# Written-out engine order at the end of a nearest-row search, a moved staging tile, and rank-order products in bf16 pieces

## The chip, the cores and the metric

The kernel runs on one core of one Trainium2 chip. The metric is device time of one execution in microseconds (us). The time before is the median of four runs: 1054.99 us (1054.68 to 1055.5). The hardware profiler took one further execution; the tables, timelines and chains quoted here are of that execution.

A core has these engines, each with its own instruction queue: PE (matrix products into PSUM, with PEld for the weight loads), DVE (vector work), ACT (activation functions and copies), POOL (GpSimd: elementwise work, and the issue of indirect transfers) and SP (which here only issues transfers). Each queue is executed in order. An instruction that waits holds up everything behind it on its own engine.

## What is computed

Four graph layers on N = 2708 nodes with D = 128 features and a dense weighted adjacency matrix A (2708 x 2708). The change touches the first two layers.

```
# layer 0
z    = leaky(d1 * (A @ (d1 * x)) @ W1 + b1)         # d1 = rowsum(A)^-1/2
S    = exp(-dist(z, z)/2), kept for the 4 nearest rows of each row
d2   = rowsum(S + A)^-1/2
x    = layernorm(x + d2 * ((S + A) @ (d2 * x)) @ W2 + b2)
# layer 1
den  = exp(leaky(r[:, None] + c[None, :]))          # r, c: one number per node
att  = den / (A @ den)
x    = layernorm(x + A @ (att @ (x @ W)))
# layers 2 and 3: two more products with A, each with a small weight and a layernorm
```

## The kernel before

**Tiling.** Rows are cut into T = 22 tiles of 128 (the last has 20 rows), columns into C = 6 chunks (four of 512, one of 384, one of 276). The first S = 16 row tiles of A are streamed through a ring buffer, the last six stay on the chip.

**The search** (L676 to L708). For each row tile PE builds 2708 keys in PSUM, ACT copies them into a `key` buffer (three buffers), and DVE takes the eight largest (`max`, L701) and their places (`max_index`, L702). Tiles go in the order 4 to 15, 0 to 3, 16 to 20; tile 21 is handled apart. A scheduler decides the order of each engine's instructions in this loop.

**The search's end.** `weigh` (L591) turns distances into weights (`sim`), sums them into the second degree, takes its inverse root `d2inv`, forms `y2 = d2inv * x`, and writes `y2` to the DRAM rows `y2_rows`. It is called for tiles 0 to 16, 17 to 19, and 20 to 21. `others` (L562) sets the own row apart from the three other near rows; it runs on POOL for the first two groups and on DVE for the last. After that, `add_bias` (L264) adds b2 to all of `xs` in one DVE instruction of 2816 elements per partition.

**Pass 2** is the product of A with `y2`, column chunk by chunk (L204 in `by_panels`). A `Due` list, which ticks once per product, says after how many products each side job is emitted; PE, DVE and ACT run in that written order. `sum_near` (L733) sums near rows of `y2`: for each tile POOL issues three indirect gathers (`gather_near`, L729) from `y2_rows`, and DVE adds them up with weights (L742). The job for tile t is due at tick 24 + 23t/5. When a chunk's product is complete and its near rows are there, `end_pass2` emits at tick n: `add_near` (L749, near rows into the same PSUM bank), a copy by ACT, the product with W2 (`norm0`, L780), normalisation, and the comparisons that rank the nodes by c (`compare` L884, `rank_rows` L902, `rank_columns` L907).

**The rank stage** (L1080 to L1475) follows. Each node has a rank in the order of c. Three things run beside each other, by a list `turns` written by hand: (1) `line` and `own_line`, products of a 32-column weight `lc` with half rows of A that are loaded into berths; when a line was used, its berth is loaded with a later one (L1032). (2) the rank-order products `in_rank_order` (L1201, output `js`): a 0/1 matrix `hot`, made on DVE by comparing (L1191), times `val_q`, which holds for each node its number and its c in f32; this sorts nodes by c. (3) `find_blocks` on DVE, then `counts` on PE (L1287), then `find_places`, then `in_list_order` (L1201, output `sl`), which gives the row lists (`slot_i`) with which POOL gathers rows of A for the attention loop, and `next_weights` for its weights `lw`. At the end `end_half(1)` copies column sums out of PSUM into the second half of the tile `heads`, and `send_half` sends them to the tile `carry` by four transfers of SP (L1389).

**The attention loop** (`block_layer`, from L1590). 44 steps; in each PE forms `num` (L1627), ACT inverts it by Ln and Exp (L1481, L1484), DVE corrects it in three instructions (L1491, L1495, L1498), and PE adds up the result (`hacc`, L1506). The buffers `inv` and `err` come from a pool that is opened after the rank stage's pool `rank` is closed, and lies where that pool lay; the first instruction that writes there waits until everything in the old pool is read, `heads` included.

Of the kernel before, what the change touches and what calls it, by code (L numbers as in the profile page):

```python
# [8 lines left out]
F32 = mybir.dt.float32  # L9
U32 = mybir.dt.uint32  # L10
I32 = mybir.dt.int32
BF16 = mybir.dt.bfloat16
# [40 lines left out]
def kernel(  # L53
# [310 lines left out]
    with tc.tile_pool(name="knn", bufs=1) as knn:  # L364
# [226 lines left out]
        def weigh(ts):  # L591

            t0, t1 = ts[0], ts[-1] + 1
            nr, sm = near[:, t0:t1, :TOPK], sim[:, t0:t1, :]

            nc.vector.tensor_add(nr, nr, nsq[:, t0:t1, None].to_broadcast([P, t1 - t0, TOPK]))
            nc.vector.tensor_scalar(nr, nr, 0.0, DIST_EPS, op0=ALU.min, op1=ALU.subtract)
            nc.scalar.activation(sm, nr, AF.Ln, scale=-1.0)
            nc.scalar.activation(sm, sm, AF.Exp, scale=0.5)
            nc.scalar.activation(sm, sm, AF.Exp, scale=-0.5)  # L600
            dd = d2inv[:, t0:t1]
            nc.vector.tensor_reduce(dd, sm, AX.X, ALU.add)
            nc.vector.tensor_add(dd, dd, deg[:, t0:t1])  # L603
            nc.scalar.activation(dd, dd, AF.Ln)
            nc.scalar.activation(dd, dd, AF.Exp, scale=-0.5)
            if t1 < T:
                nc.gpsimd.tensor_mul(
                    y2[:, t0:t1, :], xs[:, t0:t1, :], d2inv[:, t0:t1, None].to_broadcast([P, t1 - t0, D])
                )
# [5 lines left out]
            queue.dma_start(  # L615
                y2_rows[t0 * P : full * P, :].rearrange("(t p) d -> p t d", p=P), y2[:, t0:full, :]
            )
            if full < t1:
                queue.dma_start(y2_rows[FULL * P :, :], y2[:LAST, FULL, :])
            else:  # L620
                for a in range(t0, t1, 11):
                    others(range(a, min(a + 11, t1)), nc.gpsimd)
# [50 lines left out]
        tc.keep_in_program_order(nc.scalar.preload_act_table_set("natural_log_exp_and_others"))  # L673
        with tc.tile_pool(name="keys", bufs=3) as keys:

            for n, t in enumerate([*range(4, S), *range(4), *range(S, FULL)]):  # L676
# [18 lines left out]
                for c in range(C) if n else (5, 3, 2, 4, 1, 0):  # L695
# [78 lines left out]
    add_bias(b2_sb)  # L774
# [266 lines left out]
    val_q = lwx.tile([P, T, 3, NQ], F32, tag="xws", name="val_q")  # L1041
# [35 lines left out]
    with tc.tile_pool(name="rank", bufs=1) as rank:  # L1077
# [20 lines left out]

        find_ranks()
# [87 lines left out]
        def ones_at(at, n, order=iota):  # L1187
            t0, t1 = parts[n]
            w = t1 - t0
            hot = hot_in[:, n % 3 * 6 * P : (n % 3 * 6 + w) * P].rearrange("p (t k) -> p t k", k=P)  # L1190
# [15 lines left out]
        in_q = val_q[:, :, 2, :]  # L1206
# [4 lines left out]
        for n, v in enumerate((node_oob, cc)):  # L1211
            nc.vector.tensor_mul(val_q[:, :, n, :], in_q, v[:, :, None].to_broadcast(grid_q))

        places = row_tile("hot_in")
        hot_in = places[:, : 3 * 6 * P]
        two_b = places[:, 3 * 6 * P :].bitcast(BF16)[:, : T * NB].rearrange("p (t b) -> p t b", b=NB)
        assert (T * D - 3 * 6 * P) * 2 >= T * NB
        hot = [ones_at(b_j, n) for n in range(3)]

        def ranked(js):  # L1220
# [154 lines left out]
        def end_half(h):  # L1375
# [3 lines left out]
            tot = heads[:, h * span : (h + 1) * span]  # L1379
# [26 lines left out]
        def in_rank_order(n):  # L1406
            into_places(work["js"], hot[n], val_q[:, :, :2, :], n)
# [27 lines left out]
        heads = rtile([2 * span], "heads")  # L1435
# [11 lines left out]
        def own_line(n):  # L1447
# [12 lines left out]
            (next_weights,), (own_line, 1), (next_weights,), (line, 2), (next_weights,),  # L1460
            (own_line, 1), (next_weights,), (line, 1), (next_weights,), (own_line, 1), (line, 1), (next_weights,),
            (line, 1), (add_last_rows, 1), (own_line, 2),
        ]
        for f, *args in turns:
            f(*args)
        end_half(1)
# [5 lines left out]
        send_half(1, heads[:, span:], nc.sync)  # L1472
# [41 lines left out]

    m_rows = row_tile("m_rows").rearrange("p (t d) -> p t d", d=D)
    mT = m_rows.rearrange("p t d -> p (t d)")[:, :N]
# [304 lines left out]
```

## Time and profile before

| what | value |
|---|---|
| time, median of four runs | 1054.99 us |
| profiled execution: own time | 1056.77 us |
| profiled execution: span of the instructions | 1055.0 us |
| PE busy | 984.7 us, 93% |
| DVE busy | 637.3 us, 60% |
| ACT busy | 331.4 us, 31% |
| POOL busy | 264.9 us, 25% |
| mean granted TensorE clock | 0.969 |

The profiled execution lasted 1.77 us longer than its span; that is what lies before the first and after the last instruction. The stages follow each other: degrees and first product up to about 150 us of the span, the search to 290, pass 2 to about 440, the rank stage to 497, the attention loop to 720, then three products with A to the end. Shares of busy time are means over these stages, so they do not tell what an edit in one stage is worth. For that one reads, in the stage, which engine is never idle, where it does stand idle, and what ended that idle time: in a timeline this stands in brackets at the end of a line, as "[us idle <-releaser]". The granted clock is given by stretches of time as a share of full speed.

### The profile page before, as it was taken

The numbers are of one execution on the slowest core, as the hardware profiler recorded it, in microseconds if no ns is written. First come the engines' busy times: TensorE is split into PE (matmuls) and PEld (weight loads), VectorE is DVE, ScalarE is ACT, GpSimd is POOL, SyncE is SP. The second block draws the span as 40 slices with busy tenths as digits, with TensorE's granted clock in tenths as the row PEclk, the third lists the DMA queues.
The fourth block names the chain that finished last, engine by engine and source line by source line (L and its number), as shares of the span: only waits on it lengthen the run. The fifth ranks groups of instructions, "written<-read, shape, count | busy, mean of one in ns | idle before, by whom it ended". The sixth has DMA issues, their size and how long they took to land.

```text
span 1055.0 us, 11657 instructions
## 1 busy us (share of the span) xinstructions
PE 984.7 (93%) x3773; PEld 483.9 (46%) x3773; DVE 637.3 (60%) x1358; ACT 331.4 (31%) x609; POOL 264.9 (25%) x339
## 2 busy tenths in 40 slices
PE   0898999999997998799899999999999999999996
PEld 0345554444444556555333333334445544564444
DVE  5885437999954677764899999994121121122222
ACT  0000115555601244602777776662010100010000
POOL 4000000000377674007666444330121100000000
PEclk9898999999998998699899999999999999999998
DMA  9999360000075766597465556556665956585652
GB/s 339 346 365 256 97 197 1 0 1 1 1 247 194 239 176 195 195 410 232 131 181 145 141 142 160 145 160 218 217 194 171 302 176 219 146 270 163 224 173 69
DMA packets 102001, 191.00 MB, mean 181 GB/s; under 512 B 14022, under 2 KB 43342, under 8 KB 101930
## 3 DMA queue, kind: packets, MB, share of 16 engines
q1 hardware_dynamic: 83896, 152.34, 43.9%
q0 software_dynamic: 17728, 37.62, 13.0%
q8 instruction: 32, 0.52, 0.2%
q14 instruction: 39, 0.32, 0.1%
q10 hardware_dynamic: 306, 0.20, 0.1%
HBM read 214.80 MB, written 4.16 MB: 208 GB/s over the span
## 4 chain that ended last, share of the span: by engine, by line
PE 49%; DVE 1%; ACT 1%; issue 0%; POOL 0%; POOLq 0%; DVEq 0%
PE acc L204 28%; PE hacc L1506 10%; PE num L1627 10%; PE mis L285 1%; PE mis L1756 0%; DVE inv L1495 0%; DVE err L1491 0%; ACT gb L234 0%; PE mis L1722 0%; DVE inv L1498 0%; PE mis L1752 0%; POOL rstd L253 0%; PE mis L1710 0%; ACT m_rows L160 0%; DVE xs L277 0%
## 5 line engine op out<-in xcount | busy, mean ns | idle before, releaser
L1068 POOL DMA_INDIRECT ring<-in_adjT,slot_i x88 | 93.5, 1062 | 96.2 <-PE num L1627 77.4
L1627 PE MATMUL num<-ring,lw 128*64 128x512 f32 (+1 forms) x528 | 112.7, 560 | 5.1 <-DVE err L1491 4.4
L1506 PE MATMUL hacc<-inv,xws 128*128 128x512 f32 (+1 forms) x264 | 112.0, 560 | 0.3 <-DVE inv L1498 0.3
L699 PE MATMUL acc<-zT,z 128*128 128x512 f32 (+2 forms) x252 | 102.2, 552 | 0.0
L1481 ACT ACTIVATE inv<-num,plain 128x1024 f32<-128x1024 f32 x88 | 80.6, 916 | 59.5 <-PE num L1627 42.0
L253 POOL TENSOR_TENSOR rstd<-rstd,minus_half 128x4 f32<-128x4 f32 (+1 forms) x18 | 17.3, 960 | 311.8 <-DVE rstd L252 311.8
L234 ACT COPY gb<-acc 128x512 f32<-128x512 f32 (+2 forms) x18 | 9.6, 534 | 249.4 <-PE acc L204 249.4
L700 ACT COPY key<-acc 128x512 f32<-128x512 f32 (+2 forms) x126 | 67.0, 534 | 55.2 <-issue 28.0
L1506 PEld LDWEIGHTS hacc<-inv,xws 128*128 128x128 f32 x264 | 46.8, 191 | 78.0 <-issue 34.5
L204 PE MATMUL acc<-ring,y 128*128 128x512 f32 (+2 forms) x192 | 82.0, 558 | 0.5 <-issue 0.5
L1491 DVE TENSOR_TENSOR err<-inv,num 128x1024 f32<-128x1024 f32 x88 | 74.7, 854 | 10.8 <-SPq L1817 8.2
L729 POOL DMA_INDIRECT got<-y_rows,where x66 | 71.4, 1082 | 27.0 <-issue 9.1
L1498 DVE SCALAR_TENSOR_TENSOR inv<-gb,g_inv,inv 128x1024 f32<-128x1024 f32 x88 | 77.0, 914 | 0.1
L204 PE MATMUL acc<-ring,xs 128*128 128x512 f32 (+2 forms) x192 | 76.7, 543 | 0.0
L204 PE MATMUL acc<-ring,carry 128*128 128x512 f32 (+2 forms) x192 | 74.5, 542 | 0.0
L204 PE MATMUL acc<-ring,m_rows 128*128 128x512 f32 (+2 forms) x192 | 74.3, 542 | 0.0
L1495 DVE SCALAR_TENSOR_TENSOR inv<-err,inv 128x1024 f32<-128x1024 f32 x88 | 72.4, 861 | 0.1
L699 PEld LDWEIGHTS acc<-zT,z 128*128 128x128 f32 x252 | 45.9, 190 | 50.3 <-issue 44.9
L575 POOL TENSOR_TENSOR slot_e<-near,sim 128x44 f32<-128x44 f32 (+2 forms) x3 | 0.7, 242 | 270.0 <-DVE d2inv L603 267.9
L1484 ACT ACTIVATE inv<-inv 128x1024 f32<-128x1024 f32 x88 | 67.6, 768 | 2.8
L1627 PEld LDWEIGHTS num<-ring,lw 128*64 128x64 f32 x528 | 36.5, 138 | 62.5 <-issue 44.4
L701 DVE MAX8 near<-key 128x8 f32<-128x2708 f32 x21 | 62.3, 2965 | 2.6 <-ACT key L700 2.6
(376 smaller groups left out, 1374.4 us busy)
## 6 DMA issues: line engine op xcount, KB each, us to landing
ring<-in_adjT SPq DMA_DIRECT2D x74, 1024.0 KB
ring<-in_adjT SPq DMA_DIRECT2D x20, 677.0 KB
ring<-in_adjT SPq DMA_DIRECT2D x17, 768.0 KB
part<-in_adjT SPq DMA_DIRECT2D x12, 1024.0 KB
ring<-in_adjT SPq DMA_DIRECT2D x17, 552.0 KB
more<-in_adjT SPq DMA_DIRECT2D x10, 677.0 KB
res<-in_adjT SPq DMA_DIRECT2D x4, 1280.0 KB
part<-in_adjT SPq DMA_DIRECT2D x3, 768.0 KB
```

The lines of the kernel that those rows point to most:

```text
L204: nc.tensor.matmul(accs[c][: lhsT.shape[-1], :w], lhsT=lhsT, rhs=src, start=start, stop=stop)
L699: nc.tensor.matmul(pks[c][:p, : cw[c]], lhsT=z2[:, :p], rhs=zT[:, cs], start=False, stop=True)
L700: nc.scalar.copy(key[:p, cs], pks[c][:p, : cw[c]])
L729: nc.gpsimd.indirect_dma_start(out=got[:p, :], out_offset=None, in_=y2_rows[:, :], in_offset=bass.IndirectOffsetOnAxis(ap=where[:p, t, k : ...
L1068: nc.gpsimd.indirect_dma_start(out=rows[i][:KC, n, :], out_offset=None, in_=adj_half[:, :], in_offset=bass.IndirectOffsetOnAxis(ap=slot_i[ ...
L1481: nc.scalar.activation(inv, num[:, :w], AF.Ln, scale=plain[:, 0:1], bias=plain[:, 1:2])
L1484: nc.scalar.activation(inv, inv, AF.Exp, scale=-1.0)
L1491: nc.vector.tensor_mul(err, inv, num[:, :w])
L1495: nc.vector.scalar_tensor_tensor(inv, err, 2.0, inv, op0=ALU.subtract, op1=ALU.mult)
L1498: nc.vector.scalar_tensor_tensor(inv, gb[:, col : col + w], g_inv[:, q : q + 1], inv, op0=ALU.max, op1=ALU.mult)
L1506: nc.tensor.matmul(haccs[:, o:e], lhsT=xws[:, q, :], rhs=inv[:, o:e], start=(q == 0), stop=(q == NQ - 1))
L1627: nc.tensor.matmul(num[n * (BJ + 2) : (n + 1) * (BJ + 2), o:e], lhsT=lw[:, 2 * q + n, :], rhs=rows[i][:, n, c0 + o : c0 + e], start=True, ...
```

## The change

1. **The search's end.** `weigh` is cut into `weigh_near`, `find_d2` and `keep_y2`. Distances are now worked on in `sim` instead of in place in `near`. From tile 16's `max` on, DVE runs in the written order. `weigh_near` stands between a tile's `max` and its `max_index`; the rest for tiles 0 to 16 and 17 to 19 stands behind `max_index`; for tiles 20 and 21 everything up to the write of `y2` stands ahead of tile 20's `max_index`. For tiles 17 to 19, `y2` and its write are now emitted ahead of `others`.
2. **The bias.** The one addition of 2816 elements is replaced by one addition per chunk in pass 2 (`add_b2`). The due ticks of `sum_near` change from 24 + 23t/5 to 20 + 24t/5.
3. **The rank-order products.** The node number is split into two bf16 pieces and c into three (six new POOL instructions on 22 elements per partition). `val_q` becomes bf16 with five values, `hot` becomes bf16 for these products, the products are 110 columns wide instead of 44, and `ranked` adds the pieces up again (one ACT copy, three DVE instructions).
4. **The turns.** The first three rank-order products stand together, and `counts` stands after two lines instead of after eight; the lines go behind it. A few later lines and weights are in another order.
5. **The staging tile.** The second half of `heads` is no longer in the pool `rank` but in `m_rows`, a tile of the outer pool.

```diff
+                if t == T - 6:
+                    ends.enter_context(tc.manual_schedule(engines={nc.vector.engine}))
                 nc.vector.max(near[:p, t, :], key[:p])
+                if t == T - 6:
+                    weigh_near(range(0, T - 5))
+                if t == T - 3:
+                    weigh_near(range(T - 5, T - 2))
+                if t == T - 2:
+                    weigh_near(range(T - 2, T))
+                    others(range(T - 5, T - 2), nc.gpsimd)
+                    find_d2(range(T - 2, T))
+                    keep_y2(range(T - 2, T))
                 nc.vector.max_index(where[:p, t, :], near[:p, t, :], key[:p])
+                if t == T - 3:
+                    find_d2(range(T - 5, T - 2))
+                    keep_y2(range(T - 5, T - 2))
                 if t == T - 6:
-                    weigh(range(0, T - 5))
-                if t == T - 3:
-                    weigh(range(T - 5, T - 2))
-            weigh(range(T - 2, T))
+                    find_d2(range(0, T - 5))
+                    keep_y2(range(0, T - 5))
+                    for a in range(0, T - 5, 11):
+                        others(range(a, min(a + 11, T - 5)), nc.gpsimd)
             others(range(T - 2, T), nc.vector)
+            ends.close()
...
-    add_bias(b2_sb)
...
-    near_at = [24 + (23 * t) // 5 for t in range(T)]
+    near_at = [20 + (24 * t) // 5 for t in range(T)]
+    def add_b2(ts):
+        rows = xs[:, ts[0] : ts[-1] + 1, :]
+        nc.vector.tensor_add(rows, rows, b2_sb[:, None, :].to_broadcast([P, len(ts), D]))
...
+    for ts in chunk_tiles:
+        at(near_at[ts[0]], add_b2, ts)
...
-    val_q = lwx.tile([P, T, 3, NQ], F32, tag="xws", name="val_q")
+    val_q = lwx.tile([P, T, 6, NQ], BF16, tag="xws", name="val_q")
...
+        nc.gpsimd.tensor_copy(parts_b[:, :, 0], node_oob)
+        nc.gpsimd.tensor_sub(parts_b[:, :, 1], node_oob, parts_b[:, :, 0])
+        nc.gpsimd.tensor_copy(parts_b[:, :, 2], cc)
+        nc.gpsimd.tensor_sub(rest, cc, parts_b[:, :, 2])
+        nc.gpsimd.tensor_copy(parts_b[:, :, 3], rest)
+        nc.gpsimd.tensor_sub(parts_b[:, :, 4], rest, parts_b[:, :, 3])
...
-        for n, v in enumerate((node_oob, cc)):
-            nc.vector.tensor_mul(val_q[:, :, n, :], in_q, v[:, :, None].to_broadcast(grid_q))
+        grid_q = [P, T, 5, NQ]
+        nc.vector.tensor_mul(
+            val_q[:, :, :5, :], in_q[:, :, None, :].to_broadcast(grid_q), parts_b[:, :, :, None].to_broadcast(grid_q)
+        )
...
-            nc.vector.tensor_scalar_add(row_j, js[:, :NQ], float(OOB))
-            nc.vector.tensor_copy(csort, js[:, NQ : 2 * NQ])
+            nc.scalar.copy(js_sb, js[:, : 5 * NQ].rearrange("p (v q) -> p v q", q=NQ))
+            nc.vector.scalar_tensor_tensor(
+                row_j, js_sb[:, 0], float(OOB), js_sb[:, 1], op0=ALU.add, op1=ALU.add
+            )
+            nc.vector.tensor_add(csort, js_sb[:, 2], js_sb[:, 3])
+            nc.vector.tensor_add(csort, csort, js_sb[:, 4])
...
-            (line, 4), (blocks_of_edges,), (line, 7), (last_xw,), (in_rank_order, 0), (line, 3),
-            (in_rank_order, 1), (line, 3), (in_rank_order, 2), (count_lone,), (line, 2), (counts,), (line, 3),
-            (add_last_rows, 0), (own_line, 4), (ranks_known,), (line, 2), (own_line, 1), (in_list_order, 0),
+            (line, 4), (blocks_of_edges,), (line, 7), (last_xw,), (in_rank_order, 0), (in_rank_order, 1),
+            (in_rank_order, 2), (line, 2), (count_lone,), (counts,), (line, 5), (add_last_rows, 0), (own_line, 4),
+            (ranks_known,), (line, 2), (own_line, 1), (in_list_order, 0),
...
-        heads = rtile([2 * span], "heads")
+        heads = [rtile([span], "heads")]
...
+        m_rows = row_tile("m_rows").rearrange("p (t d) -> p t d", d=D)
+        mT = m_rows.rearrange("p t d -> p (t d)")[:, :N]
+        heads.append(mT[:, HALF : HALF + span])
         end_half(1)
...
-        send_half(1, heads[:, span:], nc.sync)
+        send_half(1, heads[1], nc.sync)
```

More of the change, by code (lines that the diff above doesn't have):

```diff
@@ L605, in weigh, with keep_y2 @@
             nc.scalar.activation(dd, dd, AF.Exp, scale=-0.5)
+        def keep_y2(ts):
+            t0, t1 = ts[0], ts[-1] + 1
             if t1 < T:
@@ L619, in weigh @@
                 queue.dma_start(y2_rows[FULL * P :, :], y2[:LAST, FULL, :])
-            else:
-                for a in range(t0, t1, 11):
-                    others(range(a, min(a + 11, t1)), nc.gpsimd)
         QUARTER = N // 4
@@ L673 @@
         tc.keep_in_program_order(nc.scalar.preload_act_table_set("natural_log_exp_and_others"))
+        ends = ExitStack()
         with tc.tile_pool(name="keys", bufs=3) as keys:
@@ L1097, in on_all @@
                 nc.scalar.copy(row[:, n * P : n * P + e], ps[:, :e])
+        rest = spare[:, 3 * T : 4 * T]
+        parts_b = spare[:, 4 * T : 4 * T + (5 * T + 1) // 2].bitcast(BF16)[:, : 5 * T].rearrange("p (t v) -> p t v", v=5)
+        nc.gpsimd.tensor_copy(parts_b[:, :, 0], node_oob)
[4 more added lines that the diff above has]
+        nc.gpsimd.tensor_sub(parts_b[:, :, 4], rest, parts_b[:, :, 3])
         find_ranks()
@@ L1185, with ones_at @@
         parts = [(t, min(t + 6, T)) for t in range(0, T, 6)]
-        def ones_at(at, n, order=iota):
+        def ones_at(at, n, order=None):
             t0, t1 = parts[n]
             w = t1 - t0
-            hot = hot_in[:, n % 3 * 6 * P : (n % 3 * 6 + w) * P].rearrange("p (t k) -> p t k", k=P)
+            hot = hot_b[:, t0 * P : t1 * P] if order is None else hot_in[:, n % 3 * 6 * P : (n % 3 * 6 + w) * P]
+            hot = hot.rearrange("p (t k) -> p t k", k=P)
+            order = iota if order is None else order
             nc.vector.tensor_tensor(
@@ L1204, in into_places @@
                 )
-        in_q = val_q[:, :, 2, :]
+        in_q = val_q[:, :, 5, :]
         grid_q = [P, T, NQ]
@@ L1378, in end_half @@
                 carries.append(big.tile([P, NQ * P], F32, tag="y", name="carry"))
-            tot = heads[:, h * span : (h + 1) * span]
+            tot = heads[h]
             nc.scalar.copy(tot[:, : edges[4] - edges[3]], banks[h][:, : edges[4] - edges[3]])
@@ L1406, in in_rank_order @@
         def in_rank_order(n):
-            into_places(work["js"], hot[n], val_q[:, :, :2, :], n)
+            into_places(work["js"], hot[n], val_q[:, :, :5, :], n)
             if n == 2:
```

22 lines of the change are left out of this document (12 added, 10 removed).

## The prediction

> **What bounds the kernel now.** I read the page's busy table first, then the chain that ended last, then PE's waits, then PE's timeline and the stretches around each stage that the change touches.
>
> ```profile
> PE 984.7 (93%) x3773; PEld 483.9 (46%) x3773; DVE 637.3 (60%) x1358; ACT 331.4 (31%) x609; POOL 264.9 (25%) x339
> ```
>
> PE is busy 93% of the span and nearly the whole chain lies on it. So an edit pays in two ways only: PE stands for less time, or PE's own work gets shorter; a third, hidden one is the granted clock after a stand. The change touches three places where PE stands or works slowly, A, B and C.
>
> **A, the search's end and pass 2.** The columns of a timeline are start, length, engine, line, operation, count; the bracket is the idle time ahead and its releaser. PE:
>
> ```profile
> 323.25 0.83 PE L749 MATMUL acc<-ident,near_sum 128*128 128x128 f32 x6
> 329.45 0.79 PE L749 MATMUL acc<-ident,near_sum 128*128 128x128 f32 x2 [5.37 <-DVE near_sum L742]
> 330.03 3.62 PE L204 MATMUL acc<-res,y 128*128 128x512 f32 x4
> ```
>
> PE stands 5.37 us for the sum of tile 3, which needs the twelfth gather. Behind the stand four products last 3.62, 0.91 each, and the clock of 330 to 333 was 0.50; the 4.55 us up to 334.0 lost half, 2.3. POOL and DVE tell why the gathers are late:
>
> ```profile
> 301.22 3.07 POOL L585 CAST where<-near 128x9 uint32<-128x9 f32 x1
> 304.24 0.85 POOL L615 DMA_DIRECT2D y_rows<-y  x1
> ...
> 308.45 1.15 POOL L729 DMA_INDIRECT got<-y_rows,where  x1 [2.84 <-DMA y_rows<-y]
> ```
>
> ```profile
> 301.15 3.09 DVE L265 TENSOR_TENSOR xs<-xs,b 128x2816 f32<-128x2816 f32 x1 [1.61 <-POOL y L607]
> ```
>
> The cast of nine numbers lasts 3.07 (0.20 for eighteen at 295.18) because the bias addition runs beside it; the write of `y2` for tiles 17 to 19 stands behind it on POOL, the first gather behind the write.
>
> After: `others` of tiles 11 to 16 waits for ACT, in written order now, ahead of tile 17's `max`: about 2.5 us (one key copy of 0.53 and ACT's casts) that the old order hid. With `weigh_near` ahead of the indices, tile 20's `max` goes from 290.77 to about 296.3 end, the last `y2` to 298.4, its write's issue to 299.7. With 2.5 for landing (the gathers' shortest) the first gather starts at about 302.2, not 308.45; the write for tiles 17 to 19 is out by 296. `near_sum` of tile 3 came 20.9 after the first gather, so at 323.1. PE comes to it sooner too, since the tick is 37 instead of 40: 3 ticks of 0.865 earlier, at about 321.3 with the six additions. It stands 1.8: gain 3.6. The clock fell 3 us into the old stand; I count half of the 2.3 back, 1.1. Against it: `add_b2` of the last chunks (384 elements; by the row of 2816 in 3.09 about 0.45) now stands on DVE in the chain to `xT` (L801), where PE already stands 2.64 at 414.45, and one group of rank columns, 0.5, moves ahead of chunk 5's last product: −1.0. The other `add_b2` lie in DVE's idle time beside products. **A = 3.7.** Bounds: 0.3, if the gathers start 2.3 later and the clock falls; 6.7, if the whole stand and its slow clock go.
>
> The trace shows a POOL instruction as long as the DVE instruction beside it, 3.07 against 3.09. The Trainium skill's page "SBUF — State Buffer", section "Who interferes with whom", calls this an exclusive lock: a DVE instruction with two SBUF inputs and a GpSimd instruction that reads SBUF block each other for the whole instruction. This agrees with the cast and speaks against the change, since six two-input `add_b2` now stand among the gathers: by it each could hold a gather by 0.45, up to 1.8 for the four chunks ahead of tile 3's and later ones. The rows say otherwise: 28 gathers lasted 1.00 to 1.15 although 21 two-input sums of 0.35 ran among them, so the sum takes nothing for it.
>
> **B, the rank stage.** PE has no idle time there but for 1.03 us in 453 to 456; so here PE's own work counts, and its waits for DVE.
>
> ```profile
> 455.86 1.83 PE L1201 MATMUL js<-val_q,hot_in 128*128 128x44 f32 x12
> ...
> 460.80 1.53 PE L1201 MATMUL js<-val_q,hot_in 128*128 128x44 f32 x12
> ...
> 464.10 1.53 PE L1201 MATMUL js<-val_q,hot_in 128*128 128x44 f32 x12
> ...
> 467.03 0.38 PE L1287 MATMUL cnt<-in_b,upper_b 128*128 128x484 bf16 x1
> ...
> 468.01 1.86 PE L1287 MATMUL mis<-hot_in,ones_b 128*128 128x484 bf16 x11
> 469.72 0.44 PE L1294 MATMUL mis<-hot_in,ones_b 128*128 128x44 bf16 x11
> ```
>
> The f32 products cost 1.83 + 1.53 + 1.53 + 1.21 (475.04) = 6.1 us for two passes each, 44 records. In bf16 there are 22 of one pass, 110 wide. Between 44 wide (0.04) and 484 wide (0.169) a line gives 0.06: 1.3 in all; at the 484 price 3.7. DVE, whose work stands ahead of `counts`:
>
> ```profile
> 451.05 0.66 DVE L1212 TENSOR_TENSOR val_q<-val_q,node_oob 128x484 f32<-128x484 f32 x1
> ...
> 457.77 1.23 DVE L1253 TENSOR_TENSOR in_b<-blk_b,iota_b 128x484 bf16<-128x484 bf16 x2
> ...
> 459.04 0.64 DVE L1258 TENSOR_TENSOR hot_in<-in_b 128x924 bf16<-128x924 bf16 x1
> ```
>
> Two such f32 products (1.3) become one of 22 x 5 x 22 = 2420 elements. `in_b`, bf16 with a repeated operand, ran 484 in 0.62, no faster than f32; so 2.65 by the bias row. DVE is dense from 450 on, so `two_b` (L1258) ends at 461.0 instead of 459.7. PE, with three groups of products (1.1), two lines and the lone counts, would be at `counts` by about 459.5: it waits 1.5, which is new. What is queued behind it on PE is everything: the six lines that used to run ahead. From 455.86 to the start of `counts` it was 11.17; now 5.15 with six lines (48 products, 3.9) still owed: 9.05, gain 2.1. The fourth group adds 0.9: 3.0. The clock takes some back:
>
> ```profile
> 414.00:417.00 3.00, 0.45 (x2) 0.01 (x1) 2.05 (x7) 3.00 (x6) 0.82 (x1) 0.83 0.94 342
> 417.00:420.00 3.00, 2.91 (x6) 1.92 (x7) 0.72 (x7) 0.52 (x2) 0.00 (x0) 0.50 0.34 137
> ...
> 453.00:456.00 3.00, 1.97 (x11) 1.11 (x11) 2.97 (x6) 1.07 (x6) 0.92 (x2) 1.00 1.01 419
> 456.00:459.00 3.00, 3.00 (x24) 2.12 (x28) 2.90 (x8) 0.23 (x1) 0.81 (x2) 0.66 1.02 419
> 459.00:462.00 3.00, 3.00 (x27) 1.59 (x19) 2.90 (x11) 0.00 (x0) 0.00 (x0) 0.77 1.03 415
> ```
>
> (Stretch and its length; busy time of PE, PEld, DVE, ACT, POOL; then granted clock, DMA share, GB/s.) It fell about 1.5 us into the stand of 414.45, and it fell behind 453 to 456, where PE was merely 1.97 of 3 busy, and was whole again only from about 460.8. In the changed kernel the 1.5 us stand comes just then. If the clock stays at half to 464, 1.5 goes; to 466, 2.5. I take 1.1 off: **B = 1.9.** Bounds: 4.0 (no stand: 3.0 and about 1.0), −0.9 (3.0 − 1.5 − 2.4 for products at the 484 price). POOL's six small instructions and ACT's copy of 110 columns lie beside this (both engines idle, 0.00 in 459 to 462); uncovered they cost 1.2 and 0.3. The loads that `line` issues shift with the lines; DMA share is 1.0 here, so they can only bring the late lines to a wait for data (B near 0).
>
> The Trainium skill's "TensorE: Matmul & The Clock Gate", section "What's actually happening", has the clock fall to half after an idle window of about 3.4 us. The stand of 414.45 ended after 2.64 and cost the clock, so the rows decide; by the page B would be 3.0 and the sum 10.5.
>
> **C, the attention loop's head.**
>
> ```profile
> 501.78 1.20 ACT L1481 ACTIVATE inv<-num,plain 128x1024 f32<-128x1024 f32 x1 [3.35 <-DMA res<-in_adjT]
> ```
>
> ```profile
> 497.00 3.18 SPq L1389 DMA_DIRECT2D carry<-heads  x4
> ```
>
> ```profile
> 497.08 4.32 PE L1627 MATMUL num<-ring,lw 128*64 128x512 f32 x20 [0.66 <-ACT heads L1381]
> 505.84 5.22 PE L1627 MATMUL num<-ring,lw 128*64 128x330 f32 x12 [4.44 <-DVE err L1491]
> ```
>
> The first Ln writes `inv`, which lies where `heads` lay; what it waits for is the landing of SP's four transfers out of `heads` (the releaser named, a load of `res`, is another transfer of the same queue). With `heads` in the outer pool nothing in the old pool is still read, and Ln starts when its `num` and the table load (497.15 + 1.28 = 498.43) are there: 498.85, 2.9 earlier. The same 2.9 comes off PE's 4.44, leaving 1.5. Next late is DVE's first correction, which follows Ln and Exp by 2.3. The twelve narrow products took 5.22 behind the stand against 2.50 at 513.73, so 2.7 were lost to the clock; with 1.5 us of stand some of it stays. The first `hacc` can be 2.9 + 1.95 earlier; but DVE was busy 8.84 of the 9 us from 504, and in the loop it has about 2.5 us to spare (98 to 99% in its stretches), so it cannot follow all of it. **C = 3.8**, between 2.5 (DVE sets it, some taken back) and 4.9.
>
> **Sum.** 3.7 + 1.9 + 3.8 = 9.4 off the profiled execution's own 1056.77: 1047.4. The median of the four runs is 1.78 lower than that execution: **1045.6**.
>
> **Rivals.** (1) The new wait ahead of `counts` keeps the clock low through the counts and the lines: B = −1.5, 1049.0. For it: the clock at 0.66 and 0.77 there. Against: dense lines brought it back at 460.8. (2) The written order makes DVE late and the gathers start near 307: A = −0.5, 1049.8. For it: DVE has no idle time from 266 to 298, so each wait of 2.5 moves the end. Against: the cast of 3.07 is gone in any case. (3) Loop head: DVE sets the loop, C = 1.0, 1048.4. For it: 8.84 of 9 us. Against: the chain lies on PE. (4) **Slower**: in B the clock does not come back until the list-order products, since PE now waits in small pieces (for `two_b`, then `ranks_known`). Price: each us of full-speed work at half costs one more; it decides from 11.5 us (9.4 and 2.1) of work; at 15 it gives 1060.6. For it: 430 to 445 ran at 0.50 all the way with PE 0.9 to 3.0 of 3 busy. Against: three dense stretches ended that. (5) Gains cancel, two of rivals 1 to 3 together: about 1054.
>
> **Chances.** Forecast 0.48, rivals 0.18, 0.12, 0.09, 0.08, 0.05. A measurement of this kernel tells about 0.2% (2.1 us) from no change: faster 0.87, same 0.05, slower 0.08. The range 1040.5 to 1052.0 holds the forecast's bounds (not all ends at once) and rivals 1 to 3.
>
> **What would show it.** A: the first gather at 301 to 304, a stand of 1 to 3 us ahead of `add_near`, the clock behind it at 0.8 or more. B: products of 0.06 us, a stand of 1 to 2 ahead of `counts`, the clock whole by 464. C: the first Ln released by PE, the narrow `num` behind a stand of about 1.5. I am wrong if the gathers start after 305, if PE stands over 3 ahead of `counts`, or if Ln still waits for a transfer.

## The result and the profile after

| | kernel before | changed kernel |
|---|---|---|
| median | 1055.50 us (63 runs, 1052.6 to 1064.15) | 1057.34 us (42 runs, 1053.03 to 1062.47) |
| profiled execution: own time | 1056.77 us | 1057.48 us |
| its span | 1055.0 us | 1055.7 us |
| mean granted clock | 0.969 | 0.973 |

The ratio is 1.0017, interval 1.0008 to 1.0026: the changed kernel is 0.17% slower. The forecast was 1045.6 us, faster by 0.9%. So 9.4 us of gain were forecast, and 1.8 us of loss came (0.17% of 1055): a miss of some 11 us. To see where it went, I set the same marks into both profiles (start of a first instruction on PE, or the end of the last weights product), all read from PE's timelines:

| mark, us of the span | before | after | lead of after |
|---|---|---|---|
| first product of pass 2 | 290.15 | 289.42 | 0.73 |
| first column turn of the rank stage | 439.58 | 433.08 | 6.50 |
| first rank-order product (`js`) | 455.86 | 450.08 | 5.78 |
| first list-order product (`sl`) | 478.02 | 467.65 | 10.37 |
| end of the last weights product | 493.74 | 483.91 | 9.83 |
| first `num` of the attention loop | 497.08 | 497.46 | −0.38 |
| first product behind the loop | 724.05 | 723.06 | 0.99 |
| end of the span | 1055.0 | 1055.7 | −0.7 |

Up to the last weights product the changed kernel was almost 10 us ahead. Of this, 1.95 is work that it still owed: three groups of eight line products, which the new list puts behind the weights. Even so 7.9 were left, more than the 5.6 that A and B had forecast. It lost all of that before the first `num`, in 13.55 us where the kernel before took 3.34. PE's timeline there, of the kernel before and then of the changed one:

```profile
493.67 0.78 PE L1360 MATMUL acc<-more,lc 128*32 128x339 f32 x8
494.38 0.77 PE L1370 MATMUL acc<-res,lc 20*32 20x339 f32 x8
495.08 1.34 PE L1360 MATMUL acc<-res,lc 128*32 128x339 f32 x16
```

```profile
483.84 0.78 PE L1406 MATMUL acc<-ring,lc 128*32 128x339 f32 x8
486.48 0.77 PE L1406 MATMUL acc<-ring,lc 128*32 128x339 f32 x8 [1.86 <-DMA ring<-in_adjT]
491.02 1.35 PE L1406 MATMUL acc<-more,lc 128*32 128x339 f32 x8 [3.77 <-DMA more<-in_adjT]
492.30 1.35 PE L1416 MATMUL acc<-res,lc 20*32 20x339 f32 x8
493.58 3.21 PE L1406 MATMUL acc<-res,lc 128*32 128x339 f32 x24
497.46 4.33 PE L1673 MATMUL num<-ring,lw 128*64 128x512 f32 x20 [0.67 <-ACT m_rows L1427]
```

The brackets name what was not there before: PE stands 1.86 and 3.77 us for the data of the last two lines. The rows behind the second stand are slow: eight products take 1.35 us there and 0.77 ahead of it. The stretches of the same kernel (length, busy time of PE, PEld, DVE, ACT, POOL, granted clock, DMA share, GB/s) say why:

```profile
486.00:489.00 3.00, 0.77 (x8) 0.16 (x8) 0.00 (x0) 0.00 (x0) 0.00 (x0) 1.00 0.97 248
489.00:492.00 3.00, 0.98 (x8) 0.20 (x8) 0.00 (x0) 0.00 (x0) 2.40 (x3) 0.57 0.58 128
492.00:495.00 3.00, 3.00 (x24) 0.79 (x24) 0.00 (x0) 0.00 (x0) 3.00 (x1) 0.50 0.24 75
```

From 486 to 489 PE works 0.77 us, DVE and ACT nothing, and the DMA engines are busy throughout; then the clock is at half. The sum: 5.63 of stands, about 2.3 of half clock (40 products from 491.02 to 496.79, 5.8 us; at the pace of the kernel before, 32 in 2.75, it would be 3.4), and the 1.95 owed: 9.9, against the 10.2 lost.

When were these lines asked for? SP's queue, of the kernel after and then of the kernel before:

```profile
477.33 1.61 SPq L1062 DMA_DIRECT2D ring<-in_adjT  x2
481.19 0.33 SPq L1062 DMA_DIRECT2D more<-in_adjT  x1
```

```profile
480.40 3.93 SPq L1035 DMA_DIRECT2D ring<-in_adjT  x2
484.58 1.23 SPq L1035 DMA_DIRECT2D more<-in_adjT  x1
```

These are lines 29, 30 and 31. They were issued 3 to 5 us earlier than before, while PE came to them 7 to 8 us earlier. And POOL's row gathers, which started behind all line loads in the kernel before (487.04), now start ahead of them. The kernel after:

```profile
477.05 1.07 POOL L1095 DMA_INDIRECT ring<-in_adjT,slot_i  x1 [0.30 <-DMA carry<-heads]
478.43 1.05 POOL L1095 DMA_INDIRECT ring<-in_adjT,slot_i  x1 [0.30 <-DVE lw L1392]
```

The other two places, as they look after the change. The first gather, and PE at the near sums:

```profile
298.83 0.19 POOL L585 CAST where<-near 128x9 uint32<-128x9 f32 x1
...
302.93 1.18 POOL L750 DMA_INDIRECT got<-y_rows,where  x1 [2.94 <-DMA y_rows<-y]
```

```profile
319.94 0.83 PE L770 MATMUL acc<-ident,near_sum 128*128 128x128 f32 x6
322.90 0.49 PE L770 MATMUL acc<-ident,near_sum 128*128 128x128 f32 x2 [2.13 <-DVE near_sum L763]
323.22 1.88 PE L204 MATMUL acc<-ring,y 128*128 128x512 f32 x4
```

The cast that took 3.07 takes 0.19, the gathers start 5.5 us earlier, the stand is 2.13 and the four products behind it run at full clock. Then the rank products and counts, and the loop's head on ACT and on PE:

```profile
450.08 1.04 PE L1238 MATMUL js<-val_q,hot_in 128*128 128x110 bf16 x18
...
453.50 0.36 PE L1333 MATMUL cnt<-in_b,upper_b 128*128 128x484 bf16 x1 [0.80 <-DVE in_b L1299]
454.75 0.77 PE L1333 MATMUL cnt<-hot_in,ones_b 128*128 128x440 bf16 x5 [0.88 <-DVE hot_in L1304]
...
455.71 3.34 PE L1333 MATMUL mis<-hot_in,ones_b 128*128 128x484 bf16 x11
```

```profile
499.61 1.20 ACT L1530 ACTIVATE inv<-num,plain 128x1024 f32<-128x1024 f32 x1 [0.80 <-PE num L1673]
```

```profile
503.67 0.78 PE L1673 MATMUL num<-ring,lw 128*64 128x330 f32 x4 [1.88 <-DVE err L1540]
506.54 3.79 PE L1673 MATMUL num<-ring,lw 128*64 128x512 f32 x8 [2.09 <-DMA ring<-carry]
510.26 2.54 PE L1555 MATMUL hacc<-inv,xws 128*128 128x512 f32 x6
```

Ln is released by PE now, but PE's next stand but one has a new releaser in the bracket: `ring<-carry`. On SP's queue this transfer comes behind the four out of the moved tile:

```profile
497.39 3.18 SPq L1435 DMA_DIRECT2D carry<-m_rows  x4
500.61 1.26 SPq L1523 DMA_DIRECT2D res<-in_adjT  x3
503.04 1.42 SPq L1102 DMA_DIRECT2D ring<-carry  x2
```

### The profile page after: what moved, and what is told of

It reads as the page before. It is cut to its first block, busy times and chain, and to the rows that moved or that the text cites. A ratio compares the mean times of both kernels' runs of the same rounds, so it can differ in the third digit from the quotient of the medians.

```text
span 1055.7 us, 11623 instructions
## 1 busy us (share of the span) xinstructions
PE 979.7 (93%) x3751; PEld 476.9 (45%) x3751; DVE 640.6 (61%) x1363; ACT 332.5 (31%) x610; POOL 262.7 (25%) x345
## 4 chain that ended last, share of the span: by engine, by line
PE 49%; DVE 1%; ACT 1%; issue 0%; DMA 0%; POOL 0%; POOLq 0%; DVEq 0%
PE acc L204 28%; PE hacc L1555 10%; PE num L1673 9%; PE mis L285 1%; PE mis L1802 0%; DVE inv L1544 0%; DMA ring<-carry 0%; ACT gb L234 0%; DVE err L1540 0%; PE mis L1768 0%; DVE inv L1547 0%; PE mis L1798 0%; POOL rstd L253 0%; PE mis L1756 0%; ACT m_rows L160 0%
```

## The experiments

Two theories on the 10 us that were lost ahead of the first `num` were set against each other. **Theory 1**: the new list of turns asks for the last lines too late. A berth is free when its line has been used; lines 29, 30 and 31 take the berths of lines 24, 25 and 26, and the new list puts these behind list-order and weights products. **Theory 2**: the DMA engines can't deliver the 21 lines sooner, whatever the order. Ratios are to the kernel before on the same chip, with 95% intervals.

**The parts one by one.** `old_turns` is the changed kernel with the list of before:

```diff
-            (line, 4), (blocks_of_edges,), (line, 7), (last_xw,), (in_rank_order, 0), (in_rank_order, 1),
-            (in_rank_order, 2), (line, 2), (count_lone,), (counts,), (line, 5), ...
+            (line, 4), (blocks_of_edges,), (line, 7), (last_xw,), (in_rank_order, 0), (line, 3),
+            (in_rank_order, 1), (line, 3), (in_rank_order, 2), (count_lone,), (line, 2), (counts,), ...
```

> The changed kernel with one part undone: the list of turns is that of the kernel before (counts behind eight lines, lines 24 to 26 beside the list-order products); bf16 products, search end and staging tile stay. Theory 1 (order): in the changed kernel PE was 9.8 us ahead at the last weights product and lost it all to the last three lines, since their loads wait for lines 24 to 26, which the new list puts behind weights products, and then share the DMA engines with the row gathers. With the old list those loads are issued 6 to 11 us earlier than in the kernel before, PE stands under 1 us for lines, and the time is 6 to 10 us under before, about 1047. Theory 2 (supply): the 21 line loads fill the DMA engines whatever the order, and PE only waits elsewhere: stands of 5 us or more for lines, time within 2 us of before.

`only_search` is the kernel before with parts 1 and 2 of the change alone.

> The kernel before with the search end and the bias in chunks alone (parts 1 and 2). In the changed kernel these brought PE 5.8 us ahead between the start of pass 2 and the rank stage. Theory 1 (order): nothing behind takes them back, as loads and gathers shift along: 5 to 6 us under before, about 1049.5. Theory 2 (supply): the lines take them back: within 2 us of before, with stands for line loads.

`only_staging` is the kernel before with part 5 alone:

```diff
-        heads = rtile([2 * span], "heads")
+        heads = [rtile([span], "heads")]
...
+        heads.append(mT[:, HALF : HALF + span])
         end_half(1)
...
-        send_half(1, heads[:, span:], nc.sync)
+        send_half(1, heads[1], nc.sync)
```

> The kernel before with the second half of heads in m_rows alone (part 5). The first Ln follows its num by 2.2 us instead of 4.7. Theory: the 2.5 us show at Ln, then PE stands for the transfer of carry rows into the ring at the second wide num, as in the changed kernel, and the loop in its steady state is 1.4 us earlier: 1 to 2 us under before. Rival: DVE sets the loop and the 2.5 stay whole: 2.5 or more. Second rival: the transfer takes it all: 0.

`no_rank` is the changed kernel without parts 3 and 4.

> The changed kernel with the bf16 rank-order products and the new list of turns both undone (parts 1, 2 and 5 remain). Theory 1 (order): the sum of the two kernels before it, 6.5 to 8 us under before, about 1048. Theory 2 (supply): about 1.4 under before, only what the loop's head gives.

| run | median | ratio | interval |
|---|---|---|---|
| `old_turns` | 1051.11 | 0.9964 | 0.9941 to 0.9987 |
| `only_search` | 1055.17 | 1.0010 | 0.9987 to 1.0034 |
| `only_staging` | 1054.76 | 0.9987 | 0.9966 to 1.0008 |
| `no_rank` | 1054.54 | 1.0000 | 0.9981 to 1.0018 |

With the old list the loss is gone: the last weights product ends at 485.84 and the first `num` starts at 489.18, 3.34 later as in the kernel before, and PE stands for no line longer than 0.85 us:

```profile
485.77 0.78 PE L1406 MATMUL acc<-more,lc 128*32 128x339 f32 x8
...
487.18 1.34 PE L1406 MATMUL acc<-res,lc 128*32 128x339 f32 x16
489.18 4.31 PE L1673 MATMUL num<-ring,lw 128*64 128x512 f32 x20 [0.66 <-ACT m_rows L1427]
```

For these last lines theory 2 falls: they come in time when asked for in the old order. But the gain was 0.4% where 0.6 to 0.9 was expected, and the search end and the staging tile showed next to nothing: apart, and together in `no_rank`, where the forecast had 7.5 us for them and 0.0 was measured (interval −2.0 to 1.9). So there was a second question: why do parts 1, 2 and 5 bring so little?

**What in the list costs.** `lines_up` leaves `counts` behind two lines and moves four later lines up:

```diff
-            (ranks_known,), (line, 2), (own_line, 1), (in_list_order, 0),
+            (ranks_known,), (line, 6), (own_line, 1), (in_list_order, 0),
```

and from there on it is the list of before.

> The changed kernel with counts still behind two lines, but four more lines ahead of the first list-order product, so that from there on the list of turns is that of the kernel before. Theory 1 (late loads): what costs is that lines 24 to 26, whose berths the last three loads need, stand behind weights products; with them back beside the list-order products the stands for lines (5.6 us in the changed kernel) are under 1 us, and the time is that of the old list with bf16 products, 3 to 5 us under before. Rival (early counts): counts far ahead of the lines itself costs, by its wait for DVE and the clock: time within 2 us of before or above.

`gathers_behind` is the changed kernel with one instruction more, which holds POOL's gathers until the last line is there:

```diff
+        hold = rtile([1], "hold")
+        with tc.manual_schedule(engines={nc.gpsimd.engine}):
+            nc.gpsimd.tensor_copy(hold, line_at(2 * S - 1)[:, :1])
-        load(0)
-        load(1)
+            load(0)
+            load(1)
```

> The changed kernel with one more POOL instruction: ahead of the first row gathers POOL copies one column of the last line's berth, so the gathers wait until that line has landed. Theory 1a (contention): the last loads took 7 to 10 us from issue because five row gathers ran beside them; without these they land in about 5 us, PE stands under 2 us for lines, and the first num starts near 494 in place of 497.5, since its own gathers come later. Theory 1b (issue): the loads are just issued too late; the stands stay at 4 us or more and the later gathers add to them, so first num at 500 or later, 2 us or more slower than the changed kernel.

`only_bf16` is the kernel before with part 3 alone, `only_turns` with part 4 alone.

> The kernel before with bf16 rank-order products alone (part 3), list of turns unchanged. Theory: the products are off PE's path by 4.8 us of work, DVE's longer product is covered by the lines ahead of counts; from the first of these products to the first num 2.5 to 3.5 us less, and the time 2.5 to 3.5 under before. Rival: DVE's longer product of 2420 elements makes counts late by as much: no change.

> The kernel before with the new list of turns alone (part 4), products in f32. Theory 1 (late loads): the last loads are issued later against their use here too; stands of 2 to 5 us for lines, 2 to 5 us slower than before. Rival: with f32 products PE is slow enough for the loads, within 1 us of before.

| run | median | ratio | interval |
|---|---|---|---|
| `lines_up` | 1051.02 | 0.9958 | 0.9937 to 0.9979 |
| `gathers_behind` | 1056.06 | 1.0013 | 0.9997 to 1.0030 |
| `only_bf16` | 1051.74 | 0.9962 | 0.9945 to 0.9979 |
| `only_turns` | 1067.03 | 1.0101 | 1.0071 to 1.0131 |

The list alone costs 1.0%, some 10.7 us: over twice what was expected. In its profile 10.5 us are lost between the last weights product and the first `num` (13.86 against 3.34). Its timeline on PE shows the two stands of the changed kernel nearly to the digit, and slow products behind them:

```profile
497.41 0.83 PE L1360 MATMUL acc<-ring,lc 128*32 128x339 f32 x8 [1.86 <-DMA ring<-in_adjT]
501.87 1.35 PE L1360 MATMUL acc<-more,lc 128*32 128x339 f32 x8 [3.63 <-DMA more<-in_adjT]
503.16 1.35 PE L1370 MATMUL acc<-res,lc 20*32 20x339 f32 x8
504.44 3.61 PE L1360 MATMUL acc<-res,lc 128*32 128x339 f32 x24
```

The stands are not the price of being fast: this kernel is no faster than the one before up to there (last weights product 494.85 against 493.74). `lines_up` has `counts` as early in its list as the changed kernel, and PE stands for a line once, for 1.47 (under 1 was expected); its time is that of `old_turns`:

```profile
491.68 0.78 PE L1406 MATMUL acc<-more,lc 128*32 128x339 f32 x8 [1.47 <-DMA more<-in_adjT]
```

So the early `counts` is not what costs; lines 24 to 26 behind the list order are.

`only_bf16` is 4.0 us faster by its ratio, but its profile does not put this in the rank stage: from the first rank-order product to the first `num` it took 40.0 us against 41.2 before, since PE stood for earlier lines with the DMA engines full (share 1.01 to 1.03 from 452 to 461):

```profile
456.92 0.78 PE L1379 MATMUL acc<-ring,lc 128*32 128x339 f32 x8 [2.44 <-DMA ring<-in_adjT]
458.58 0.78 PE L1379 MATMUL acc<-more,lc 128*32 128x339 f32 x8 [0.31 <-DMA more<-in_adjT]
460.23 0.78 PE L1379 MATMUL acc<-more,lc 128*32 128x339 f32 x8 [0.87 <-DMA more<-in_adjT]
```

So ahead of `counts` theory 2 holds in part: there a faster PE also meets lines that have not landed. Another 5.4 us of this profile lie in pass 2 (143.99 from its start to the first column turn, against 149.43 before), where the two programs are the same; one profile can't price a part there.

In `gathers_behind` PE's timeline has

```profile
489.67 0.78 PE L1406 MATMUL acc<-more,lc 128*32 128x339 f32 x8 [2.32 <-DMA more<-in_adjT]
...
494.08 1.04 PE L1676 MATMUL num<-ring,lw 128*64 128x512 f32 x2 [1.09 <-DMA ring<-in_adjT,slot_i]
...
499.42 1.08 PE L1676 MATMUL num<-ring,lw 128*64 128x512 f32 x4 [1.12 <-DMA ring<-in_adjT,slot_i]
```

One stand of 2.32 in place of 5.63: the last load came 6.3 us after its issue, not 9.8. So in this pair of profiles the gathers beside the loads made up over half of the stands and the late issue the rest; I had expected under 2. The first `num` came at 494.08, near the 494 of theory 1a. The time is no better, since PE now stands for the gathers: the first product behind the loop came 227.5 us after the first `num`, against 225.6 in the changed kernel.

**Search end and staging tile again.** Three edits on `old_turns`. `two_queues`:

```diff
-                queue.dma_start(
+                (queue or (nc.sync, nc.scalar)[g % 2]).dma_start(
...
-        send_half(1, heads[1], nc.sync)
+        send_half(1, heads[1], None)
```

> The run with the old list of turns, and of the four transfers of the second half of heads two issued by ACT instead of all four by SP. Theory: the loop's head is set by SP's queue, where these four (3.2 us), three loads of res and a branch stand ahead of the transfer of carry rows into the ring that the wide num of step 2 needs; that num stands ahead of the first hacc on PE. With two of them on ACT this transfer is issued 1.6 us earlier, PE's stands for it (1.0 and 1.1 us) vanish, the first hacc comes about 10.5 us behind the first num in place of 11.9, and the time is 1 to 1.5 us less. Rival: the row gathers of step 2 or DVE set it: the first hacc stays at 11.9 or later.

`late_near`:

```diff
-        n = max(due.n + 1, near_at[chunk_tiles[c][-1]] + 3, ended[-1] + 16)
+        n = max(due.n + 1, near_at[chunk_tiles[c][-1]] + (9 if c == 0 else 3), ended[-1] + 16)
```

> The run with the old list of turns, with near_sum of the first chunk added to its bank six ticks later (tick 43 in place of 37). Theory: the search end brought the gathers 3 us forward, but PE reaches the near sums 2.6 us earlier too, so that it still stands 4 to 5 us and then works 3.4 to 6.8 us at half clock. At tick 43 PE has products to do while the gathers run: no stand over 1.5 us, no half clock there, and 3 to 5 us less from the start of pass 2 to the first column turn of the rank stage (147.1 in the run it is built on). Rival: the near sums' later place makes what hangs on them late (column turns, the chain to xT), no gain.

Both of these, and `old_turns` without parts 1 and 2:

> The two changes before together on the run with the old list of turns. Theory: the gains add, 4 to 6 us under that run, 0.990 to 0.992 of the kernel before.

> The run with the old list of turns, with the search end and the bias as in the kernel before (parts 3 and 5 remain). Theory: the search end is worth 1.7 us at most as it stands, since its stand and half clock remain: 0 to 2 us slower than the run with the old list, 0.996 to 0.998 of the kernel before. Rival: it is worth the 5.8 us of the changed kernel's profile: 1.000 or above.

On the chip of these four the kernel before took 1078.7 us, and `two_queues`, `late_near`, `both_late` and `no_search` had 0.9894 (0.9861 to 0.9927), 0.9915 (0.9882 to 0.9948), 0.9894 (0.9858 to 0.9929) and 0.9881 (0.9840 to 0.9923): no difference among them, so the later near sums showed no gain here (`both_late` against `two_queues`). Their profiles are longer in pass 2, 159 to 164 us to the first column turn where the other runs have 143 to 150. In three of the four a late copy of ACT is the reason, here in `two_queues`:

```profile
335.63 0.58 ACT L1000 COPY hT<-acc 128x512 f32<-128x512 f32 x1 [34.97 <-remote]
```

ACT's copy came 13 us after its input, and PE stood 12.33 us for it; 14.00 and 15.50 in `late_near` and `both_late`. In `no_search` this copy is not late, and PE stands 6.18 and 3.39 elsewhere in pass 2. What held ACT is not in the trace, and why the kernel before is slow on this chip isn't shown. The loop's head can still be read: in `two_queues` the stands for `ring<-carry` are gone, but ACT's two issues took 1.59 us and a further 1.0 passed before the table load, so that Ln came 1.72 us later behind `num` and PE stood 3.59 for `err`. The first `hacc` was 11.33 behind the first `num`, against 11.89 in `old_turns` and 10.36 in `late_near` on the same chip, which leaves all four transfers on SP: no gain.

So `old_turns` as the base, the kernel without parts 1 and 2 and the one with later near sums were measured again on one chip, with a fourth that has part 5 undone:

> The run with the old list of turns once more, as the base for the other three on one chip: 0.996 of the kernel before, as in its first measurement (0.994 to 0.999).

> The same without the search end and the bias in chunks (A). Theory: A is worth under 2 us, since PE still stands for the near sum of tile 3 and the half clock follows: 0.996 to 0.998 of the kernel before, stage from pass 2 to the first column turn 149 us against 147. Rival: A is worth the 5.8 us of the changed kernel's profile: 1.000 or above.

> The same without the moved half of heads (C). Theory: C is worth nothing that can be measured, since the transfers that the first Ln used to wait for also stand ahead of the carry rows that the num of step 2 needs: within 0.1% of the base, the end of the loop as far behind the first num as with C (225 to 227 us). Rival: C is worth the 2.6 us by which Ln is earlier: 0.25% above the base.

> The same as the base, with the near sums of the first chunk six ticks later. Theory: no stand of more than 1.5 us ahead of add_near, no half clock behind it, 3 to 5 us less from pass 2 to the first column turn and 0.3% less time than the base. Rival: no gain, what hangs on the near sums comes late.

| run | median | ratio | interval | pass 2 to first column turn, us |
|---|---|---|---|---|
| `old_turns_again` | 1050.57 | 0.9952 | 0.9934 to 0.9971 | 146.93 |
| `no_search_again` | 1050.81 | 0.9972 | 0.9956 to 0.9988 | 148.43 |
| `no_staging` | 1051.45 | 0.9974 | 0.9958 to 0.9990 | 147.16 |
| `late_near_again` | 1044.07 | 0.9910 | 0.9883 to 0.9938 | 143.30 |

By the middle of the intervals, search end and staging tile are worth 2.1 and 2.3 us, by the medians 0.2 and 0.9; the intervals overlap, so neither is shown apart from zero. `late_near_again` is the fastest kernel of this study, 0.9% under the kernel before and by the two ratios 1.1% under the changed one. Against the base on its chip it gains 4.4 us by the ratios and 6.5 by the medians, with six executions against twelve; the intervals just overlap, and the chip before had shown no gain. PE in the base, and then in `late_near_again`:

```profile
317.89 0.83 PE L770 MATMUL acc<-ident,near_sum 128*128 128x128 f32 x6
322.89 0.49 PE L770 MATMUL acc<-ident,near_sum 128*128 128x128 f32 x2 [4.17 <-DVE near_sum L763]
323.22 2.82 PE L204 MATMUL acc<-ring,y 128*128 128x512 f32 x4
```

```profile
321.32 2.74 PE L204 MATMUL acc<-res,y 128*128 128x512 f32 x6
323.90 1.05 PE L770 MATMUL acc<-ident,near_sum 128*128 128x128 f32 x8
324.79 1.88 PE L204 MATMUL acc<-res,y 128*128 128x512 f32 x4
```

The base stands 4.17 us and then runs at half clock for 3.4; six ticks later the sums are there when PE comes, and it does not stand for them.

## Why the prediction was wrong

**The step that failed** is in B: "The loads that `line` issues shift with the lines; DMA share is 1.0 here, so they can only bring the late lines to a wait for data (B near 0)." The place was seen, the sum counted nothing for it, and the worst that this sentence allowed was a B near 0. The loads do not shift with PE as a whole, but with the lines that free their berths, and the new list moves lines 24 to 26 behind the list-order products. I followed the six lines that go behind `counts`, and not the four fewer lines ahead of the list order. In place of B = 1.9 the profile showed −6.2: from the first rank-order product to the first `num` 47.4 us against 41.2. With the list of before it was 38.4 to 38.7 in the profiles of `old_turns`, `old_turns_again`, `no_search_again` and `no_staging`. By the ratios the new list costs 5.6 us (`old_turns`) to 6.2 (`lines_up`) in the changed kernel, and 10.7 in the kernel before (`only_turns`). It was no help elsewhere: `lines_up`, `old_turns` and `only_bf16` agree within their intervals. Of my rivals, the one in the rank stage had the clock stay low behind `counts`, the slower one had it fall in small waits up to the list order. Neither was it: behind `counts` the clock was at half for 3.4 us, from 455.3. None of the three signs that I had named came either (gathers at 302.9, 0.80 ahead of `counts`, Ln released by PE): none of them looked at a load.

That is about half of the miss. The other half is that A and C were counted at 7.5 and measured between 0.0 together (`no_rank`) and 4.4 in sum, one by one (`no_search_again`, `no_staging`).

**B, what else it said.** Right: 18 products took 1.04 us, 0.058 each (forecast 0.06), DVE's product of 2420 elements 2.68 (2.65), and the stand ahead of `counts` and within them was 0.80 + 0.88 (1.5). The half clock behind it cost 1.5 us in the changed kernel (3.34 for eleven products that took 1.86), and nothing in `lines_up`, with stands of 1.49 and 0.88; the forecast of 1.1 lies between the two. The bf16 products with the list of before shorten this stage by 2.6 to 2.9 us in these four profiles and by 1.2 in `only_bf16`, whose ratio has 4.0; the terms for products and list together came to 1.9.

**A, right in mechanism, too large.** The cast is short, the gathers still wait for the write of `y2`, and they start at 302.9 (forecast 302.2). This nearness is in part luck: pass 2 began 0.73 earlier. Counted from the start of pass 2 this is 13.5 us in the changed kernel and 13.4 to 15.4 in the other runs with the new search end, where I had 12.05: the first gather came 3.9 us behind the end of the last write's issue in the changed kernel (issued until 299.0) and 5.1 in `only_search` (298.4), where I took 2.5 for landing. Since the tick had been moved from 40 to 37, PE came to the sums 2.6 us earlier as well, so the stand was 4.2 to 4.7 in most runs with the new search end (forecast 1.8; 5.8 in two pieces in `lines_up`), and the half clock came with it. The changed kernel's own profile, with 2.13 and no half clock, is the exception: 143.66 from pass 2 to the first column turn, where the others with the new search end at tick 37, but for those with the late copy of ACT, have 146.9 to 149.8. That such a profile also comes by chance shows in `only_bf16`: it has the old search end and 143.99, where the other runs with the old one, but for the slow `no_search`, have 148.4 to 149.4. The three `add_b2` of 0.68 that fall among the first 32 gathers did not hold them: these lasted 0.99 to 1.26, near the 1.00 to 1.15 of before. The term of 3.7 measured 0 to 2. `late_near_again` got what I had counted on, by letting PE come later.

**C, the wait moved.** Ln starts 2.15 behind the first `num` in place of 4.70, released by PE: as forecast. What I did not follow is what else hangs on the four transfers of `heads`. On SP they stand ahead of the carry rows that step 2's `num` needs, and in PE's written order this `num` stands ahead of the first `hacc`. So PE stands 1.88 for DVE and then 2.09 for `ring<-carry`. The first `hacc` came 12.8 behind the first `num`, against 13.9 before: 1.1 of the 4.85 that I had as the upper end. At the loop's end the gain does not stand out: the first product behind it came 224.2 to 227.6 us after the first `num` in the runs with the moved tile, and 225.8 to 227.0 in those without. The term of 3.8 measured 1.4 alone (`only_staging`, interval across zero) and 2.3 on `old_turns` (0.9 by the medians).

The range ended at 1052.0, and with the list of before the kernel would have lain in it (1051.11 and 1050.57). A slower kernel was only in the slower rival, and that rival had the wrong cause.

## What to carry to other kernels

When the order of work changes, follow each buffer's release, not only the instructions: the load that refills it moves with the last reader, and a list that makes one chain early makes the readers it passes late. A stand is the difference of two times; to bring the data some 3 us forward and the consumer 2.6 us forward leaves most of the stand, and moving the consumer back was worth more (4.4 us on one chip) than the whole restructuring ahead of it (0 to 2). A wait taken off one engine should be followed to the next user of the same transfer before it is counted as gained.

## What the runs showed of the hardware

The clock's records have half-speed stretches of 3.4, 6.8, 10.2, 13.7 and 17.1 us and of nothing between, apart from the one cut off by the end: multiples of one window of 3.4 us. The Trainium skill's "TensorE: Matmul & The Clock Gate", section "What's actually happening", names a window of about that length; this agrees with its length, not with the idle time needed, since the clock fell in the stand of 2.64 ahead of L852 (2.65 ahead of L872 after) in both profiles. In `only_bf16` the same stand, ended at 413.19, left it whole:

```profile
412.00:415.00 3.00, 1.81 (x7) 1.37 (x8) 0.68 (x4) 1.62 (x4) 0.00 (x0) 1.00 0.68 271
```

In the changed kernel stands of 1.7 in sum at `counts` were followed by half clock, and 2.4 there in `lines_up` were not. So one and the same stand may cost nothing, or half of what runs in 3.4 or 6.8 us behind it.

It also fell without a stand. In the changed kernel's last product:

```profile
958.00:961.00 3.00, 3.00 (x14) 1.82 (x14) 1.20 (x6) 0.00 (x0) 0.00 (x0) 0.91 0.00 0
961.00:964.00 3.00, 3.00 (x5) 1.05 (x4) 2.10 (x14) 0.00 (x0) 0.42 (x1) 0.52 0.00 0
```

PE is busy throughout, and still 0.52. This took 1.7 us off the changed kernel's lead of 0.99; in the kernel before, which does the same work there, the clock was 1.00. It came in six of the sixteen profiles of the experiments, `only_turns` and `only_search` among them, so it belongs to no part of the change. In all seven the half clock begins 2.6 to 4.9 us behind the start of the products of the last row tile, which has 20 rows (955.66 in the changed kernel); whether these are the cause, no run tests. Single executions of one kernel spread far more than the parts are worth: twelve of `old_turns_again` went from 1043.9 to 1052.6 us. That is why the parts worth 2 us could not be told from zero.
